# One more buffer for running totals in a causal attention kernel, paid for with smaller tiles of inverses

## The chip, the cores and the metric

The kernel runs on one core of one Trainium2 chip. The metric is device time in microseconds (us) from start to end of one launch, as the median of several runs.

## The reference, cut to what matters

```python
# x: (32, 256, 32, 32) f32; 8 heads of 32 channels, S = 1024 positions
xn = group_norm(x, 32 groups)
q, k, v = 1x1 convolutions of xn              # 256 channels each, with bias
scores = einsum('bhqd,bhkd->bhqk', q, k) / sqrt(32)
attn = softmax(where(k < q, scores, -1e4)); attn = where(k < q, attn, 0)
out = x + einsum('bhqk,bhkd->bhqd', attn, v)
```

## The kernel before: the parts that matter

A batch is one image. It is worked off in N = 12 visits. A visit multiplies q and k into `sT` (in PSUM, the on-chip memory for products; these are the score products), ScalarE takes exponentials of `sT` into the tiles `e` and `eh` (in SBUF, the on-chip memory for tiles), GpSimd masks the diagonal blocks, and one visit later TensorE multiplies them with v into `acc`. The heads come in two groups of four and the queries in two halves of 512, so a batch has four pairs, n = 0 to 3. The first exponentials of a pair go to a tile with tag `e0`, and VectorE adds all later ones of the pair onto it: this tile is the running total.

```python
epool = tc.alloc_tile_pool(name="epool", bufs=3)
...
tag = "e0" if full[2] == 0 else "e"        # k == 0: visits 0, 2, 6, 8 of a batch
e = epool.tile([P, 4, HALF], F32, tag=tag, name=f"{tag}_{name}")      # 8 KB a partition, 3 buffers
```

The 128 rows of a total are folded to 64 and then 32 by two adding DMAs issued on GpSimd. A plain DMA from SP's queue, called the stacking here, puts those 32 rows into `folded`; one product then sums all four pairs of the image. Only when the stacking has landed can the total's buffer be used again.

```python
def fold(b, n, rows):
    total = live["sum", b, *divmod(n, NH)]
    nc.gpsimd.dma_start(out=total[:rows], in_=total[rows : 2 * rows], accum_op=ALU.add)

def stack(b, n):
    if n == 0:
        live["folded", b] = work.tile([P, 4, HALF], F32, tag="folded", bufs=1, ...)
    total = live.pop(("sum", b, *divmod(n, NH)))
    nc.sync.dma_start(out=live["folded", b][n * HD : (n + 1) * HD], in_=total[:HD])
...
SUMS = (3, 7, 9, 13)                        # visit behind which pair n's first fold is asked for
PREPARE = (-18, -17, -16, -15, -14, -12, -11, -11)   # norm of an image: ..., mean, deviation, variance, ...
with tc.manual_schedule(engines={ENG.PE, ENG.Activation, ENG.DVE, ENG.Pool}):   # SP is not among them
    ...
    when(v, lambda b=b, n=n: fold(b, n, 2 * HD), after)
    when(v + 2, lambda b=b, n=n: fold(b, n, HD), after)
    when(v + 3, lambda b=b, n=n: stack(b, n), after)
    ...
    when(first + N + 6, lambda b=b: sum_folded(b), after)
```

`when(i, f)` runs f in visit i between its scores and its values, `after` behind its values; v is the visit behind which pair n's first fold is asked for (3, 7, 9, 13). The inverses of the sums come back from DRAM into `rb`, which also takes the finished output:

```python
live["rb", b] = work.tile([P, NG, S], F32, tag="rb", name=f"rb_{b}")    # 8 KB a partition, 2 buffers
```

Of the kernel before, what the change touches and what calls it, by code (L numbers as in the profile page):

```python
# [9 lines left out]
F32 = mybir.dt.float32  # L10
I32 = mybir.dt.int32
AF = mybir.ActivationFunctionType
# [5 lines left out]
P = 128  # L18
# [13 lines left out]
def tile_norm_attention_residual(  # L32
# [77 lines left out]
    def unshifted():  # L110
# [190 lines left out]
        def scores(b, full, half):  # L301


            tag = "e0" if full[2] == 0 else "e"
            name = f"{b}_{full[0]}_{full[1]}_{full[2]}"
            e = epool.tile([P, 4, HALF], F32, tag=tag, name=f"{tag}_{name}")
            eh = epool.tile([P, 4, HALFBANK], F32, tag="eh", bufs=4, name=f"eh_{name}")
            pairs = [ps_s.tile([P, 2, HALF], F32, tag="sT", name=f"sT_{name}_{a}") for a in range(3)]
            short = pairs[2].rearrange("p bank (n q) -> p bank n q", n=2)
            first = [scores_of((b, half), short[:, j % 2, 1, :], j) for j in (2, 3)]  # L310
            for j in range(4):
                scores_of((b, full), pairs[j // 2][:, j % 2, :], j)

            for ins in first:
                ins.then_inc(bank_free, 1)
                tc.no_tile_sem_insts.add(ins.ins.name)
            live["free"] = live.get("free", 0) + len(first)
            wait = nc.tensor.wait_ge(bank_free, live["free"])
            for ins in first:
                tc.declare_no_dep(wait.ins, ins.ins, reason="the semaphore orders them")  # L320
            for j in range(2):
                lo = scores_of((b, half), short[:, j, 0, :], j)
                for ins in first:
                    tc.declare_no_dep(lo.ins, ins.ins, reason="the semaphore orders them")
            for a in range(2):
                nc.scalar.activation(e[:, 2 * a : 2 * a + 2, :], pairs[a], AF.Exp)  # L326
            exp = nc.scalar.activation(eh.rearrange("p (n bank) q -> p bank n q", n=2), short, AF.Exp)  # L327

            for ins in first:
                tc.add_to_no_dep_group(f"first_{name}", ins.ins)  # L330
                tc.add_to_no_dep_group("first", ins.ins)
            tc.declare_no_dep(exp.ins, group=f"first_{name}", reason="through the last two products")
            tc.declare_fence(exp.ins, group=f"first_{name}")
            mask(full, e)
            mask(half, eh)
            live["e", b, full], live["e", b, half] = e, eh
# [30 lines left out]
        def stack(b, n):  # L367
            if n == 0:
                live["folded", b] = work.tile([P, 4, HALF], F32, tag="folded", bufs=1, name=f"folded_{b}")
            total = live.pop(("sum", b, *divmod(n, NH)))  # L370
            nc.sync.dma_start(out=live["folded", b][n * HD : (n + 1) * HD], in_=total[:HD])
# [64 lines left out]
        def invert(b, ns):  # L436
            part = slice(ns.start * HD, ns.stop * HD)
            inv = small.tile([P, ROW], F32, tag="inv", name=f"inv_{b}_{ns.start}")
            nc.vector.reciprocal(inv[part], live["rows", b][part])
            live["inv", b] = dram.tile([4, 4, HALF], F32, tag="inv", name=f"inverses_{b}_{ns.start}")  # L440
            nc.sync.dma_start(out=spread_rows(live["inv", b])[part], in_=inv[part])
            if ns.start == 0:
                live["rb", b] = work.tile([P, NG, S], F32, tag="rb", name=f"rb_{b}")
            by_half = live["inv", b] if b >= B - 2 else live["inv", b].rearrange("j n c -> n j c")
            for n in ns:
                g, hf = divmod(n, NH)
                nc.sync.dma_start(
                    out=live["rb", b][:, g, hf * HALF : (hf + 1) * HALF],
                    in_=by_half[n].unsqueeze(1).broadcast_to([4, HD, HALF]),
                )  # L450

        def finish(b, n, within=slice(0, HALF)):
            g, hf = divmod(n, NH)
            cols = slice(hf * HALF + within.start, hf * HALF + within.stop)
            num, rb, xt = live["num", b, n], live["rb", b], live["x", b]
            nc.vector.tensor_mul(rb[:, g, cols], num[:, within], rb[:, g, cols])  # L456
            nc.vector.scalar_tensor_tensor(  # L457
                rb[:, g, cols], rb[:, g, cols], v_bias_col[:, g : g + 1], xt[:, g, cols], ALU.add, ALU.add
            )
            if cols.start == 0:  # L460
                nc.vector.tensor_copy(rb[:, g, 0:1], xt[:, g, 0:1])
            nc.sync.dma_start(out=x_out[b, :, g, cols], in_=rb[:, g, cols])

        def check_here(n, ok):

# [3 lines left out]
            nc.vector.scalar_tensor_tensor(ok, live["most", n], SUM_MAX, least, ALU.is_le, ALU.mult)  # L469

        def invert_here(b, n, within):
            g, hf = divmod(n, NH)
            nc.vector.reciprocal(
                live["rb", b][:, g, hf * HALF + within.start : hf * HALF + within.stop], live["den", n][:, within]
            )

        def finish_aside(b, n):

            g, hf = divmod(n, NH)
            cols = slice(hf * HALF, (hf + 1) * HALF)  # L480
            num, rb, xt = live["num", b, n], live["rb", b], live["x", b]
            nc.gpsimd.tensor_tensor(rb[:, g, cols], num, rb[:, g, cols], ALU.mult)
            nc.gpsimd.tensor_tensor(rb[:, g, cols], rb[:, g, cols], xt[:, g, cols], ALU.add)
            nc.scalar.activation(rb[:, g, cols], rb[:, g, cols], AF.Identity, bias=v_bias_col[:, g : g + 1])
            if hf == 0:
                nc.scalar.copy(rb[:, g, 0:1], xt[:, g, 0:1])
            nc.sync.dma_start(out=x_out[b, :, g, cols], in_=rb[:, g, cols])

        def end_last(b):

# [33 lines left out]
        def when(i, f, where=at):  # L524
            where.setdefault(i, []).append(f)
# [22 lines left out]
        with tc.manual_schedule(engines={ENG.PE, ENG.Activation, ENG.DVE, ENG.Pool}):  # L548
# [23 lines left out]
            for b in range(B):  # L572
                first, last, late = b * N, b == B - 1, b >= B - 2
                if b >= 1:
                    for n, f in zip(PROJECT if not last else PROJECT[:-1] + (8,), projections(b)):
                        when(first + n, f)
                if b >= 2:
                    when(max(first - 2 * N + 3, 0), lambda b=b: load(b))
                    prepare(b, [first + n for n in PREPARE])
                for n in every:  # L580
                    v = first + (N if last and n == 3 else SUMS[n])
                    if last and n == 3:
                        for i in (N - 1, N):
                            when(first + i, lambda b=b, i=i: sum_pieces(b, products[i - 1], i == N - 1, i == N), after)
                    if late:
                        when(v, lambda b=b, n=n: sums(b, *divmod(n, NH)), after)
                    else:
                        when(v, lambda b=b, n=n: fold(b, n, 2 * HD), after)
                        when(v + 2, lambda b=b, n=n: fold(b, n, HD), after)
                        when(v + 3, lambda b=b, n=n: stack(b, n), after)  # L590
                if not last:
                    if not late:
                        when(first + N + 6, lambda b=b: sum_folded(b), after)
                    v = first + N + (2 if late else 8)
                    when(v, lambda b=b: gather(b, every))
                    when(v + 2, lambda b=b: check_sums(b, every))
                    when(v + 2, lambda b=b: invert(b, every))
                    for n in every:
                        when(first + FINISH[late][n], lambda b=b, n=n: finish(b, n), after)
                else:  # L600
                    when(first + N - 4, lambda b=b: gather(b, every[:2]))
                    when(first + N - 3, lambda b=b: check_sums(b, every[:2]))
                    when(first + N - 3, lambda b=b: invert(b, every[:2]))
                    when(first + N, lambda b=b: check_here(2, in_range[:, ROW : ROW + 1]))
                    when(first + N, lambda b=b: invert_here(b, 2, slice(0, HALF)))
                    when(first + N, lambda b=b: finish(b, 2))
                    for n in every[:2]:
                        when(first + N, lambda b=b, n=n: finish_aside(b, n), after)
# [167 lines left out]
```

## Time and profile before

| | before |
|---|---|
| median of the first three runs | 2074.72 us (2067.27 to 2076.96) |
| span of the profiled run | 2070.3 us |
| granted TensorE clock, mean | 0.958 |
| busy PE, DVE, ACT, POOL | 94%, 75%, 68%, 38% |

PE is TensorE's products, DVE is VectorE, ACT ScalarE, POOL GpSimd, SP the engine whose queue issues most DMAs. The page also gives the chain of work that ended last, as shares of the span by engine:

```profile
PE 62%; DMA 15%; ACT 8%; DVE 5%; POOL 5%; issue 4%; ACTq 0%; SPq 0%; POOLq 0%; DVEq 0%
```

Although PE is busy for 94% of the span, only 62% of the chain is PE's. Nearly all of the rest is a path around PE: masks, folds, stacking, exponentials.

### The profile page before, as it was taken

The numbers are of one execution on the slowest core, as the hardware profiler recorded it, in microseconds if no ns is written. First come the engines' busy times: TensorE is split into PE (matmuls) and PEld (weight loads), VectorE is DVE, ScalarE is ACT, GpSimd is POOL, SyncE is SP. The second block draws the span as 40 slices with busy tenths as digits, with TensorE's granted clock in tenths as the row PEclk, the third lists the DMA queues.
The fourth block names the chain that finished last, engine by engine and source line by source line (L and its number), as shares of the span: only waits on it lengthen the run. The fifth ranks groups of instructions, "written<-read, shape, count | busy, mean of one in ns | idle before, by whom it ended". The sixth has DMA issues, their size and how long they took to land.

```text
span 2070.3 us, 54028 instructions
## 1 busy us (share of the span) xinstructions
PE 1954.0 (94%) x23410; PEld 966.5 (47%) x23410; DVE 1562.8 (75%) x1604; ACT 1412.3 (68%) x1775; POOL 794.9 (38%) x741
## 2 busy tenths in 40 slices
PE   8999999999999999899999999999999999999996
PEld 4544444454444444445444454444444444544443
DVE  4787688777777877778777786787877777777767
ACT  5767676776667776667766676766776667766675
POOL 2444343442434434334343342443443434424323
PEclk9999999999999999999999999999999999999998
DMA  3555656656666556565556655656566555565412
GB/s 110 83 99 105 121 125 133 110 109 116 124 124 112 118 109 124 124 123 103 110 121 127 115 105 115 127 123 130 110 111 124 119 129 109 113 114 124 94 46 74
DMA packets 77660, 233.54 MB, mean 113 GB/s; under 512 B 19825, under 2 KB 20977, under 8 KB 62057
## 3 DMA queue, kind: packets, MB, share of 16 engines
q0 software_dynamic: 15360, 94.39, 33.9%
q1 hardware_dynamic: 60280, 134.72, 21.4%
q8 instruction: 185, 3.03, 0.7%
q10 hardware_dynamic: 1776, 0.92, 0.2%
q14 instruction: 59, 0.48, 0.1%
HBM read 68.54 MB, written 35.62 MB: 50 GB/s over the span
## 4 chain that ended last, share of the span: by engine, by line
PE 62%; DMA 15%; ACT 8%; DVE 5%; POOL 5%; issue 4%; ACTq 0%; SPq 0%; POOLq 0%; DVEq 0%
PE sT L279 22%; PE acc L349 15%; PE pp L171 11%; PE ppv L171 11%; DMA folded<-e 8%; DMA e<-e 6%; ACT e L326 6%; DVE e L354 4%; POOL e L294 2%; PE pd L384 2%; POOL eh L294 2%; ACT eh L327 2%; ACT k L233 1%; POOL rstd L209 1%; DVE rb L456 1%
## 5 line engine op out<-in xcount | busy, mean ns | idle before, releaser
L326 ACT ACTIVATE e<-sT 128x1024 f32<-128x1024 f32 x768 | 745.8, 1023 | 552.5 <-PE sT L279 325.6
L354 DVE TENSOR_TENSOR e<-e,eh 128x1024 f32<-128x1024 f32 x382 | 540.9, 1430 | 455.0 <-PE acc L349 429.8
L279 PE MATMUL sT<-q,k 32*128 32x256 f32 (+3 forms) x7168 | 679.9, 480 | 77.6 <-ACT e L326 76.8
L294 POOL TENSOR_SCALAR_AFFINE_SELECT e<-e 128x512 f32<-128x512 f32 (+1 forms) x256 | 365.5, 1428 | 877.1 <-ACT e L326 847.1
L354 DVE TENSOR_TENSOR e<-e,e 128x1536 f32<-128x1536 f32 x381 | 628.9, 1651 | 24.1 <-POOL e L294 3.0
L279 PEld LDWEIGHTS sT<-q,k 32*128 32x128 f32 x7168 | 478.2, 190 | 282.6 <-ACT e L326 96.6
L171 PE MATMUL pp<-xn,wT 128*32 128x512 f32 x4096 | 492.3, 598 | 0.0
L349 PE MATMUL acc<-e,v 128*32 128x512 f32 (+2 forms) x4096 | 400.7, 486 | 0.0
L327 ACT ACTIVATE eh<-sT 128x1024 f32<-128x1024 f32 x384 | 396.6, 1033 | 0.0
L365 POOL DMA_DIRECT2D e<-e x240 | 197.3, 861 | 363.7 <-DMA e<-e 227.6
L171 PE MATMUL ppv<-wT,xn 128*32 128x256 f32 x4096 | 274.3, 413 | 0.0
L349 PEld LDWEIGHTS acc<-e,v 128*32 128x32 f32 x4096 | 132.5, 110 | 224.8 <-issue 202.6
L349 PE MATMUL acc<-eh,v 128*32 128x256 f32 x3072 | 224.1, 379 | 0.0
L171 PEld LDWEIGHTS pp<-xn,wT 128*32 128x32 f32 x4096 | 107.0, 109 | 218.5 <-issue 205.6
L171 PEld LDWEIGHTS ppv<-wT,xn 128*32 128x32 f32 x4096 | 128.2, 118 | 134.5 <-issue 63.2
L294 POOL TENSOR_SCALAR_AFFINE_SELECT eh<-eh 128x512 f32<-128x512 f32 x128 | 178.3, 1393 | 0.4
L349 PEld LDWEIGHTS acc<-eh,v 128*32 128x32 f32 x3072 | 97.5, 110 | 165.3 <-issue 153.3
L456 DVE TENSOR_TENSOR rb<-num,rb 128x512 f32<-128x512 f32 (+1 forms) x127 | 110.9, 873 | 0.1
L457 DVE SCALAR_TENSOR_TENSOR rb<-rb,v_bias_col,x 128x512 f32<-128x512 f32 (+1 forms) x127 | 96.1, 757 | 4.5
L249 ACT COPY v<-ppv 128x512 f32<-128x512 f32 x128 | 77.3, 604 | 26.2 <-PE ppv L171 26.2
L233 ACT ACTIVATE q<-pp,qk_bias 128x512 f32<-128x512 f32 x128 | 89.8, 702 | 4.7 <-PE pp L171 4.7
L233 ACT ACTIVATE k<-pp,qk_bias 128x512 f32<-128x512 f32 x128 | 89.6, 700 | 2.2 <-PE pm L171 1.1
(69 smaller groups left out, 501.6 us busy)
## 6 DMA issues: line engine op xcount, KB each, us to landing
e<-e POOLq DMA_DIRECT2D x120, 512.0 KB, 7.9
x<-in_x_dram SPq DMA_DIRECT2D x64, 512.0 KB
out_dram<-rb SPq DMA_DIRECT2D x127, 256.0 KB
rb<-inverses SPq DMA_DIRECT2D x126, 256.0 KB
e<-e POOLq DMA_DIRECT2D x120, 256.0 KB, 4.6
folded<-e SPq DMA_DIRECT2D x120, 256.0 KB
rows<-sums SPq DMA_DIRECT2D x31, 32.0 KB
inverses<-inv SPq DMA_DIRECT2D x31, 32.0 KB
```

The source lines that it names most:

```text
L171: nc.tensor.matmul(out[part], lhsT=lhsT[:, part], rhs=rhs, start=start, stop=stop, skip_group_check=True)
L233: nc.scalar.activation(live[key][:, cols], pp, AF.Identity, bias=qk_bias[:, n, g : g + 1], scale=(SCALE, 1.0)[n],)
L249: nc.scalar.copy(live["v", b][:, 2 * n : 2 * n + 2, :], pp)
L279: ins = nc.tensor.matmul(pair[:, cols], lhsT=live["k", b, g][rows, kb * P : (kb + 1) * P], rhs=live["q", b, g][rows, hf * HALF + of.start ...
L294: nc.gpsimd.affine_select(out=diagonal, in_=diagonal, pattern=[[0, 4], [0, n], [1, P]], compare_op=ALU.is_gt, fill=0.0, base=0, channel_mu ...
L326: nc.scalar.activation(e[:, 2 * a : 2 * a + 2, :], pairs[a], AF.Exp)
L327: exp = nc.scalar.activation(eh.rearrange("p (n bank) q -> p bank n q", n=2), short, AF.Exp)
L349: nc.tensor.matmul(acc[HD * j : HD * (j + 1), of], lhsT=live["v", b][:, kb, h * HD : (h + 1) * HD], rhs=e[:, j, cols], start=first, stop=l ...
L354: nc.vector.tensor_add(total[:, :, of], total[:, :, of], e[:, :, cols])
L365: nc.gpsimd.dma_start(out=total[:rows], in_=total[rows : 2 * rows], accum_op=ALU.add)
L456: nc.vector.tensor_mul(rb[:, g, cols], num[:, within], rb[:, g, cols])
L457: nc.vector.scalar_tensor_tensor(rb[:, g, cols], rb[:, g, cols], v_bias_col[:, g : g + 1], xt[:, g, cols], ALU.add, ALU.add)
```

## The change

It gives the running totals a fourth buffer (8 KB a partition). Room for it comes from `rb`: a tile of 2 KB for each pair, four of them, instead of two tiles of 8 KB for a whole image. And it asks for each stacking two visits behind the second fold (`v + 4`), not one (`v + 3`, after the values). Without the smaller `rb` the fourth buffer doesn't fit; the build then says that its pool needs 72 KB a partition and 71.06 are left.

```diff
-            e = epool.tile([P, 4, HALF], F32, tag=tag, name=f"{tag}_{name}")
+            e = epool.tile([P, 4, HALF], F32, tag=tag, bufs=4 if tag == "e0" else 3, name=f"{tag}_{name}")
...
-            if ns.start == 0:
-                live["rb", b] = work.tile([P, NG, S], F32, tag="rb", name=f"rb_{b}")
...
+        def inverses(b, n):
+            live["rb", b, n] = work.tile([P, HALF], F32, tag="rb", bufs=4, name=f"rb_{b}_{n}")
+            return live["rb", b, n]
...            (finish, invert_here and finish_aside use live["rb", b, n] in the same way)
-                        when(v + 3, lambda b=b, n=n: stack(b, n), after)
+                        when(v + 4, lambda b=b, n=n: stack(b, n))
```

## The prediction

> **What bounds the kernel now.** I read the page first, then the waits, the chain, PE's timeline around one wait, and last the sums over chosen windows. The page puts PE first, and the granted clock at full almost everywhere:
>
> ```profile
> PE 1954.0 (94%) x23410; PEld 966.5 (47%) x23410; DVE 1562.8 (75%) x1604; ACT 1412.3 (68%) x1775; POOL 794.9 (38%) x741
> ```
>
> PE is the bound. Its missing 6% and the half-speed time hidden in its busy time are what can be won. The table of waits, over the whole span, says what it waits for:
>
> ```profile
> ACT e L326 <- DMA folded<-e: 179.9, 33, 8.8
> PEld sT L279 <- ACT e L326: 96.6, 57, 5.8
> PE sT L279 <- ACT e L326: 76.8, 38, 5.5
> ```
>
> Read them backwards. PE's score products wait for PSUM that the exponentials free; the exponentials wait, 33 times, some once a batch (32 images), for the DMA that stacks a running total's 32 rows into `folded` (the stacking). Only then is the total's buffer free for the next one. In the chain of waits one such event looks like this (start, length, what):
>
> ```profile
> 1035.84 1.62 POOL eh L294
> 1037.46 7.21 DMA e<-e
> ...
> 1044.80 6.82 DMA folded<-e
> ...
> 1051.72 1.03 ACT e L326
> ...
> 1052.80 3.84 PE sT L279 x12
> ```
>
> The second fold (an adding DMA issued by GpSimd) takes 7.21 us, the stacking 6.82 us, the exponential 1.03 us, and then PE goes on. PE's timeline shows the price:
>
> ```profile
> 1052.80 3.91 PE L279 MATMUL sT<-q,k 32*128 32x256 f32 x16 [3.85 <-ACT e L326]
> 1056.64 2.95 PE L171 MATMUL ppv<-wT,xn 128*32 128x256 f32 x32
> ...
> 1061.24 1.57 PE L279 MATMUL sT<-q,k 32*128 32x256 f32 x16
> 1062.74 1.93 PE L171 MATMUL ppv<-wT,xn 128*32 128x256 f32 x32
> ```
>
> PE stood for 3.85 us, and then the same two groups took 3.91 and 2.95 us where one visit later they take 1.57 and 1.93. The wait is paid twice: as idle time and as a slow restart.
>
> **Which wait it is.** A batch has 12 visits (each starts with a group of score products in PE's timeline). A running total starts at visits 0, 2, 6, 8. With three buffers, the total of visit 2 takes the one of the previous batch's visit 6, whose folds are due after visits 9 and 11 and whose stacking after visit 12, which is this batch's visit 0. So the stacking has two visits to land, and it doesn't. The trace agrees: the wait ends before the scores of visit 3, and once, in the batch from 1544.83, there is one at visit 6 instead.
>
> **What the Trainium skill says.** "TensorE: Matmul & The Clock Gate", Part 1, has the array run at half clock after an idle window of some 3.4 us and return after a busy one. The trace agrees on the restart: 0.89 is granted in the idle window below and 0.55 in the 6.60 us after it. It also pays after shorter waits; see the batch mean below. "DMA: Bandwidth & Descriptors", Issuing engines are not separate DMA queues, says that all transfers run on the same 16 engines and interleave. The trace agrees: the DMA share is 0.68 and then 1.02 around the wait, against 0.53 for the rest of the batch (windows below); that is why 256 KB of stacking needs 6.82 us. "Perfetto Trace Analysis", DMA Instruction — HWDGE, says that the movement is not in the reported time of the issue; so I read landings from who waits.
>
> **The change part by part.** Windows: us, then busy time (instructions) of PE, PEld, DVE, ACT, POOL, then granted clock, DMA share, GB/s.
>
> ```profile
> 80.45:138.39 57.94, 57.56 (x732) 29.23 (x728) 42.12 (x41) 43.81 (x55) 24.52 (x24) 1.00 0.50 78
> 138.39:1929.27 1790.88, 1701.61 (x20389) 839.76 (x20385) 1368.91 (x1401) 1228.53 (x1540) 704.98 (x645) 0.96 0.60 118
> ...
> 1048.90:1052.80 3.90, 0.05 (x5) 0.00 (x1) 3.87 (x6) 1.08 (x2) 0.79 (x1) 0.89 0.68 204
> 1052.80:1059.40 6.60, 6.60 (x48) 3.20 (x52) 1.05 (x2) 5.68 (x7) 0.80 (x1) 0.55 1.02 196
> 1059.40:1113.90 54.50, 54.12 (x684) 27.04 (x676) 43.78 (x44) 37.15 (x47) 23.39 (x21) 1.00 0.53 101
> ```
>
> The first window is batch 1, which has no such wait, at full clock: 57.94 us. The second holds 28 batches (2 to 29): 1790.88 / 28 = 63.96 us each. So the wait with its restart costs 63.96 - 57.94 = 6.02 us a batch; the single event above costs 3.85 + (3.91 + 2.95 - 1.57 - 1.93) = 7.2 us, and some are smaller.
>
> 1. *Fourth buffer.* Each total now takes the buffer of the same total a batch ago. The slack from stacking to reuse becomes 5, 3, 5 and 3 visits of some 4.8 us, even with the stacking put one visit later. Measured from the second fold's issue (1037.46) to the stacking's landing (1051.62) there are 14.2 us, under three visits, so I expect the wait gone in all batches. Gain: 28 x 6.02 = 168.6 us, and in batch 30, whose visits 2 and 3 I read from PE's timeline as 6.34 and 8.64 us against 4.22 and 5.09 in batch 1, another 5.7 us. Sum 174.3 us.
> 2. *Room.* `rb` goes from 2 x 8 KB to 4 x 2 KB, the new total costs 8 KB: even. The number and size of instructions and transfers stay; a half's `rb` is used from visit 10 to visit 2 of the next batch, and its slot is asked for again at visit 10. No wait; 0 us. Only the end, where inverses of the last image are wanted two visits after the image before, could wait a little: I take 1 us.
> 3. *Stacking later.* No instruction is added. A stacking waits on SP for its fold anyway; it now stands behind some loads of inverses and some output stores in that in-order queue, so it may land some us later, inside the new slack. 0 us.
>
> What stays: DVE has 48.8 us of work a batch (1562.8 us over 32 batches), 84% of 57.94; ACT has 44.1 us, 76%.
>
> **Rivals.** *A. The sum product becomes the wait.* After visit 6 PE multiplies `folded`, so it needs the stacking of the last total, issued in visit 3 or 4 among image loads and stores. Today the stall before it gives it time. The batch that lost the stall shows how near it is (ACT's, SP's and PE's timelines):
>
> ```profile
> 1577.77 1.94 ACT L326 ACTIVATE e<-sT 128x1024 f32<-128x1024 f32 x2 [3.77 <-DMA folded<-e]
> 1566.93 16.93 SPq L371 DMA_DIRECT2D folded<-e  x2
> 1581.25 1.93 PE L384 MATMUL pd<-folded,pick_half 128*32 128x512 f32 x8 [2.48 <-ACT k L233]
> ```
>
> That stacking was issued at 1566.93 and landed at 1577.77, after 10.8 us; PE was ready for the sum product at 1581.25 - 2.48 = 1578.77, 1.0 us later. (It waited there through ACT, which stood at visit 6; the fourth buffer removes that.) This batch still lost 6.20 - 5.09 = 1.1 us at visit 3, so without it the margin is about nothing. For: the product stays at its visit, and the change makes nothing of the last total's path shorter. Against: it costs only the overlap. I take 0.4 us a batch, 28 x 0.4 = 11 us. If stackings land 1.5 us later, with some half-clock restarts, it is 50 to 60 us, and the time about 1955.
>
> *B. DVE becomes the bound.* For: 84% busy, and its finishing work lies in visits 0 to 3, where the stall used to let it catch up. Against: in that same batch without a stall at visit 2 it was waiting for PE again by 1563.98, before visit 4. I give it 0; if it came, 1 us a batch, about 1935.
>
> *C. The wait shifts to another transfer or to GpSimd*, which stands 7 us in front of the second fold with masks behind it. For: 227.6 us of its waits are for the folds. Against: visits 2 and 3 have no masks, and in that batch GpSimd was free at 1563.45, visit 4's mask came at 1567.85. If it took back half the gain, the time would be near 1990.
>
> **Range and chances.** 2074.7 - 174.3 + 1 + 11 = 1912. The floor without any new wait is 1901 and some noise; hence the low end 1893. Rival A at twice to four times my size gives 1925 to 1945, the upper end. Nothing in the change adds work, so slower is nearly excluded; within 2% (above 2033) would need over two thirds of the gain given back.
>
> **What would show each step right or wrong.** Right: the waits of ACT for `folded` gone or under 10 us; batches 2 to 29 at 58 to 59 us; no score product waiting more than 1 us for ACT; granted clock above 0.98; busy time of DVE, ACT and POOL the same, PE's down by the restarts (some 80 us). Rival A shows as idle before the sum product, once a batch, and cold visits at 7. B shows as values or exponentials waiting for DVE's sums, C as exponentials or values waiting for GpSimd. The prediction is wrong if the exponentials still wait for `folded`, most likely because a stacking behind other entries of SP's queue comes more than three visits late.

## The result

| | before | changed |
|---|---|---|
| median of 4 runs | 2075.84 us (2067.27 to 2077.10) | 1901.83 us (1901.16 to 1902.73) |
| span of the profiled run | 2070.3 us | 1900.5 us |
| granted clock, mean | 0.958 | 0.997 |
| PE busy | 1954.0 us (94%) | 1860.3 us (98%) |

The ratio of times is 0.917, with a 95% interval of 0.9145 to 0.9196. Ratios here are the mean time of one kernel's runs over that of the other's of the same rounds, so they aren't quite the ratio of the quoted medians. The kernel before varies by about 1.5% from run to run in the studies below (2053 to 2083 us), the changed one by some 0.3%.

From the page of the changed kernel, the busy times and the chain:

```profile
PE 1860.3 (98%) x23410; PEld 944.9 (50%) x23410; DVE 1569.0 (83%) x1604; ACT 1410.1 (74%) x1775; POOL 802.5 (42%) x741
...
PE 89%; ACT 5%; DMA 2%; issue 2%; DVE 1%; POOL 0%; ACTq 0%; POOLq 0%; SPq 0%; DVEq 0%
```

PE executes the same 23410 products in 93.7 us less busy time; busy time before included products that ran at half clock. By the trace's record of the granted clock, which is 0.5 or 1.0 at any moment, PE was busy during 148 of the 174 us at half clock, so the clock accounts for at most half of that, 74 of the 93.7 us (an estimate from this record). The DMA's share of the chain fell from 15% to 2%. The table of waits no longer has the line of exponentials waiting for `folded`; these are what is left of it and beside it:

```profile
ACT e L326 <- PE sT L279: 359.7, 347, 1.8
...
PE pm L171 <- ACT k L233: 11.4, 30, 0.4
...
PE pd L384 <- DMA folded<-e: 1.1, 3, 0.5
```

The exponentials now wait mostly for PE, so ScalarE follows PE and not the reverse. PE itself still stands 0.38 us once a batch before the product that gives the means (`pm`), and now and then shortly before the product over `folded` (`pd`).

PE's timeline, in one batch, at visits 2 (612.58), 3 (616.80) and 4 (621.88); compare the restart that the prediction shows:

```profile
612.58 1.57 PE L279 MATMUL sT<-q,k 32*128 32x256 f32 x16
614.08 1.92 PE L171 MATMUL pp<-xn,wT 128*32 128x512 f32 x16
615.82 1.05 PE L349 MATMUL acc<-e,v 128*32 128x384 f32 x16
616.80 1.57 PE L279 MATMUL sT<-q,k 32*128 32x256 f32 x16
618.30 1.93 PE L171 MATMUL ppv<-wT,xn 128*32 128x256 f32 x32
```

No line has an idle time before it, and the score products take 1.57 us. The window of batches 2 to 29, with the columns that the prediction explains:

```profile
138.02:1764.48 1626.46, 1612.32 (x20388) 818.76 (x20385) 1375.92 (x1401) 1226.46 (x1540) 713.30 (x645) 1.00 0.66 130
```

1626.46 / 28 = 58.09 us a batch, against 63.96 before.

All later readings of visits come from PE's timeline: a visit starts with its first score product, twelve make a batch. These are means over batches 2 to 29, in us, of each kernel's profiled run:

| kernel | batch | visit 2 | visit 3 | visit 6 | clock |
|---|---|---|---|---|---|
| before | 63.96 | 6.88 | 8.24 | 5.85 | 0.958 |
| changed | 58.09 | 4.22 | 5.09 | 5.81 | 0.997 |
| `rb_alone` | 63.47 | 6.73 | 7.95 | 5.83 | 0.964 |
| `four_stack_soon` | 58.14 | 4.22 | 5.09 | 5.87 | 0.996 |
| `three_fold_sooner` | 62.29 | 5.74 | 7.42 | 6.17 | 0.979 |
| `hold8` | 59.33 | 4.23 | 6.47 | 5.67 | 0.997 |
| `hold14` | 64.29 | 6.85 | 8.80 | 5.67 | 0.958 |
| `hold20` | 66.55 | 9.46 | 8.46 | 5.67 | 0.942 |

Of the 6.02 us a batch over 57.94, the kernel before lost 2.66 in visit 2, 3.15 in visit 3 and 0.18 in visit 6. The changed kernel has visits 2 and 3 at their floor in each of these batches, and visit 6 takes 0.14 us more than its floor of 5.67.

### The profile page after: what moved, and what is told of

Same layout as the page of the kernel before. It is cut to its first block, busy times and chain, and to the rows that moved or that the text cites. A ratio compares the mean times of both kernels' runs of the same rounds, so it can differ in the third digit from the quotient of the medians.

```text
span 1900.5 us, 54083 instructions
## 1 busy us (share of the span) xinstructions
PE 1860.3 (98%) x23410; PEld 944.9 (50%) x23410; DVE 1569.0 (83%) x1604; ACT 1410.1 (74%) x1775; POOL 802.5 (42%) x741
## 4 chain that ended last, share of the span: by engine, by line
PE 89%; ACT 5%; DMA 2%; issue 2%; DVE 1%; POOL 0%; ACTq 0%; POOLq 0%; SPq 0%; DVEq 0%
PE sT L279 29%; PE acc L349 24%; PE pp L171 21%; PE ppv L171 12%; ACT e L326 2%; PE pd L384 2%; ACT eh L327 1%; DMA folded<-e 1%; ACT k L233 1%; DVE e L354 0%; PE pm L171 0%; DMA wn<-in_L_conv_kv_w_dram 0%; DVE rb L472 0%; DVE rb L457 0%; DVE rb L458 0%
## 5 line engine op out<-in xcount | busy, mean ns | idle before, releaser
L294 POOL TENSOR_SCALAR_AFFINE_SELECT e<-e 128x512 f32<-128x512 f32 (+1 forms) x256 | 387.1, 1512 | 698.1 <-ACT e L326 673.9
L354 DVE TENSOR_TENSOR e<-e,e 128x1536 f32<-128x1536 f32 x381 | 638.4, 1676 | 25.0 <-POOL e L294 4.0
L279 PE MATMUL sT<-q,k 32*128 32x256 f32 (+3 forms) x7168 | 617.5, 460 | 0.8 <-ACT k L233 0.8
L279 PEld LDWEIGHTS sT<-q,k 32*128 32x128 f32 x7168 | 463.4, 184 | 170.5 <-ACT q L233 50.6
L365 POOL DMA_DIRECT2D e<-e x240 | 197.4, 862 | 364.8 <-DMA e<-e 205.9
L171 PE MATMUL ppv<-wT,xn 128*32 128x256 f32 x4096 | 247.3, 382 | 0.0
L171 PEld LDWEIGHTS ppv<-wT,xn 128*32 128x32 f32 x4096 | 120.2, 109 | 102.0 <-issue 32.1
L294 POOL TENSOR_SCALAR_AFFINE_SELECT eh<-eh 128x512 f32<-128x512 f32 x128 | 164.0, 1281 | 1.1
L357 ACT COPY num<-acc 128x512 f32<-128x512 f32 x128 | 76.4, 597 | 15.9 <-PE acc L349 15.9
```

What stands on the lines that cost most here:

```text
L171: nc.tensor.matmul(out[part], lhsT=lhsT[:, part], rhs=rhs, start=start, stop=stop, skip_group_check=True)
L279: ins = nc.tensor.matmul(pair[:, cols], lhsT=live["k", b, g][rows, kb * P : (kb + 1) * P], rhs=live["q", b, g][rows, hf * HALF + of.start ...
L294: nc.gpsimd.affine_select(out=diagonal, in_=diagonal, pattern=[[0, 4], [0, n], [1, P]], compare_op=ALU.is_gt, fill=0.0, base=0, channel_mu ...
L354: nc.vector.tensor_add(total[:, :, of], total[:, :, of], e[:, :, cols])
L357: nc.scalar.copy(num, acc)
```

## The experiments

The theory: the gain is the removal of one wait, that of the exponentials for a total's buffer, and the wait was paid as idle time and again as a slow restart. The rivals: the smaller tiles or the place of the stacking did something; the slow products came of crowded DMAs; more buffers weren't needed, only an earlier fold.

### `rb_alone`: everything but the fourth buffer

```diff
-bufs=4 if tag == "e0" else 3
+bufs=3
-                        when(v + 4, lambda b=b, n=n: stack(b, n))
+                        when(v + 3, lambda b=b, n=n: stack(b, n), after)
```

> The changed kernel with three buffers of totals and the old place of the stacking: only the smaller tiles of inverses are left of the change. Theory (the fourth buffer is the whole gain): 2076 us, within 1% of the kernel before; exponentials wait some 180 us for folded again. Rival (the smaller tiles free something): clearly under 2050 us.

Measured: 2068.72 us, ratio 1.0012 (0.9944 to 1.0081), the same as the kernel before. Its table of waits has the old line:

```profile
ACT e L326 <- DMA folded<-e: 168.7, 32, 9.0
```

The smaller tiles change nothing measurable by themselves. They are the room and nothing else.

### `four_stack_soon`: the fourth buffer, the stacking in its old place

```diff
-                        when(v + 4, lambda b=b, n=n: stack(b, n))
+                        when(v + 3, lambda b=b, n=n: stack(b, n), after)
```

> The changed kernel with the stacking asked for where the kernel before had it, after visit v+3. Built, its order of instructions and waits on every engine is the same as that of the changed kernel but for buffer numbers. Theory: the place of that line does nothing, 1902 us within 0.3%. Rival (the prediction's part 3, that the stackings move behind loads and stores in SP's queue): the stackings' issue times differ by some us, and the time by a few us.

Measured: 1903.25 us, ratio 0.9184 (0.9132 to 0.9235); the changed kernel's is 0.917. Comparing the built instruction lists engine by engine, I found this kernel and the changed one the same in order and waits, and SP's order of transfers the same in the kernel before as well; the traces agree, with the same order of SP's 539 transfers, by tile names, in all three. SP isn't among the engines whose order the source fixes, so moving the line by a visit moved no instruction. The prediction had said that the stackings would now stand behind loads of inverses and stores in SP's queue. The third total's stacking does, behind four such loads and one store, but it stood there in the kernel before already.

### `hold8`, `hold14`, `hold20`: the wait rebuilt without a DMA

These are the changed kernel with idle copies put in ScalarE's queue ahead of visit 2's exponentials, in batches 2 to 29. Nothing waits for a buffer; the exponentials are just late.

```diff
+        held = const.tile([P, HALFBANK], F32, name="held")
+        def hold(count):
+            for _ in range(count):
+                nc.scalar.copy(held, wT[:, 0, :HALFBANK])
...
+                if 2 <= b < B - 2:
+                    when(first + 1, lambda: hold(8), after)      # 14, 20 in the others
```

> The changed kernel with 8 copies of 128x256 put on ScalarE ahead of visit 2's exponentials in batches 2 to 29, some 0.3 us each, 2.4 us in all: about 1.2 us more than the idle time that stands there. Theory and rival alike: that fits into the room before PE waits, under 10 us in all, 1902 to 1912 us. It fixes the zero of the two longer holds.

> 14 such copies, some 4.2 us, 3.0 us over the idle time there. Theory (a wait of PE is paid twice, as idle time and as a restart at half clock): PE stands about 1 us a batch and in part of the batches some 3 us of slow restart follow; 1950 to 2020 us. Rival (only the idle time is paid): 1902 + 28 x 1 = 1930 us, clock as before near 1.

> 20 such copies, some 6 us, 4.8 us over the idle time there. Theory: PE stands about 3 us a batch, and then some 3.3 us go to half clock; 1902 + 28 x 6.3 = 2078 us, granted clock near 0.96, the kernel before over again without any DMA in it. Rival (the slow restart came of the crowded DMA or of something else in the kernel before): idle alone, 1902 + 28 x 3 = 1986 us, clock near 0.99.

Measured: `hold8` 1934.87 us (ratio 0.9364), `hold14` 2072.88 (1.0029), `hold20` 2137.10 (1.0341). The copies were longer than I had reckoned: 8 took 3.49 us and 14 took 6.10 by ScalarE's timeline, some 0.44 us each and not 0.3. So each hold is larger than its expectation assumed, and all three missed their numbers; `hold14`, with 4.59 us of delay as measured below, came out where `hold20` had been expected (4.8 us, 2078 us). Counted from the start of visit 2, the first exponential of it begins at 1.19 us in the changed kernel and at 3.16, 5.78 and 8.39 in the three, delays of 1.97, 4.59 and 7.20 us. In the kernel before it begins at 5.79 us on average, as in `hold14`, which was luck and makes the two easy to compare. The cost a batch over 57.94 us is 1.39, 6.35 and 8.61.

PE's timeline in `hold8`, at visit 3:

```profile
624.02 0.70 PE L279 MATMUL sT<-q,k 32*128 32x256 f32 x4
624.93 2.04 PE L279 MATMUL sT<-q,k 32*128 32x512 f32 x12 [0.21 <-ACT e L326]
626.90 1.93 PE L171 MATMUL ppv<-wT,xn 128*32 128x256 f32 x32
```

And in `hold14`:

```profile
666.78 0.70 PE L279 MATMUL sT<-q,k 32*128 32x256 f32 x4 [2.56 <-ACT e L326]
667.69 2.99 PE L279 MATMUL sT<-q,k 32*128 32x512 f32 x12 [0.21 <-ACT e L326]
670.61 3.64 PE L171 MATMUL ppv<-wT,xn 128*32 128x256 f32 x32
```

In `hold8` the score products are strung out along the exponentials: they take 624.02 to 626.90, 2.88 us, instead of 1.50, with hardly a gap to be seen, and the next products run at full speed (1.93 us for 32). The clock stays at 0.997. In `hold14` PE stands 2.56 us as well and afterwards the same 32 products take 3.64 us. The windows of its wait and of the 6.83 us from 667.54 (clock, DMA share and GB/s are the last three numbers) show why:

```profile
664.22:666.78 2.56, 0.00 (x2) 0.00 (x1) 2.56 (x4) 2.46 (x6) 0.00 (x0) 1.00 0.89 201
667.54:674.37 6.83, 6.68 (x48) 3.12 (x52) 1.58 (x3) 4.97 (x8) 1.34 (x2) 0.50 0.91 122
```

The half clock is granted after the wait. Over batches 2 to 29 the clock record has such stretches, of 3.41 or 6.83 us each, in every batch of `hold14`, in 26 of the 28 of the kernel before and in none of `hold8`. In `hold14` the cost exceeds the delay, 6.35 against 4.59 us. From `hold14` to `hold20` it rises by 2.26 us for 2.61 us of delay, so the restart is not paid again. The mean clock still falls, to 0.942, because more of the half clock falls into the wait itself: PE was busy during 168 of its 232 us, against 159 of 160 in `hold14`. So the mean clock alone is no measure of the cost.

`hold14` has the fourth buffer and no wait for any DMA, and yet its time (ratio 1.0029 to the kernel before), its clock (0.958) and its visits 2 and 3 are nearly those of the kernel before. So neither the number of buffers nor a wait for a DMA is needed for the slow products; a late exponential does it. The DMA engines were crowded there too (0.91), so `hold14` alone doesn't rule out that crowding slows the products. The window of one stacking in the kernel before speaks against it:

```profile
1044.80:1051.62 6.82, 4.15 (x48) 1.86 (x48) 6.73 (x10) 0.00 (x0) 0.28 (x1) 1.00 0.92 228
```

At a DMA share of 0.92 and a clock of 1.00, the score products at 1044.66 took 1.57 us and the 16 products behind them 1.92, as in the changed kernel.

### `three_fold_sooner`: three buffers, the one fold a visit earlier

```diff
-bufs=4 if tag == "e0" else 3
+bufs=3
-                        when(v + 2, lambda b=b, n=n: fold(b, n, HD), after)
-                        when(v + 4, lambda b=b, n=n: stack(b, n))
+                        when(v + (1 if n == 2 else 2), lambda b=b, n=n: fold(b, n, HD), after)
+                        when(v + (2 if n == 2 else 3), lambda b=b, n=n: stack(b, n), after)
```

> Three buffers, but the second fold of the third total (started at visit 6) is asked for one visit earlier, and its stacking with it. Theory (it is the lateness of that one stacking, not the count of buffers as such): the stacking is issued some 6 us sooner and the wait at visits 2 and 3 goes. What is left is the next one in line with three buffers, the stacking of the last total before visit 6, some 3 us short as in the batch at 1544.83 of the kernel before; so batches of 59.5 to 62 us, 1945 to 2015 us in all, 1975 as the point. Rival (the fold itself would be as late, because GpSimd's queue or the shared DMA engines set it): no change, 2060 to 2090 us.

Measured: 2023.89 us, ratio 0.9785 (0.9726 to 0.9844), just outside what I expected and a quarter of the gain (the interval excludes 1). Its waits still have a large line:

```profile
ACT e L326 <- DMA folded<-e: 156.7, 41, 9.8
```

The fold was issued when I had reckoned: on average 10.7 us after visit 9 begins instead of 16.8, and the stacking followed at 17.5 instead of 23.8. But it landed at 28.4 instead of 29.7, by the landings that the trace records. Its way took 10.9 us instead of 5.9. SP's timeline shows what it stands behind now:

```profile
1009.29 4.15 SPq L444 DMA_DIRECT2D rb<-inverses  x4
1013.64 1.68 SPq L371 DMA_DIRECT2D folded<-e  x1
1021.01 10.82 SPq L461 DMA_DIRECT2D out_dram<-rb  x4
```

Directly ahead of it are the four loads of inverses, 1 MB in all; in the kernel before they were issued 10 us or more earlier (1031.82 to 1034.38, the stacking at 1044.80). That these loads cost the 5 us is argued from this order; no run moved them, and none issued the stacking from another engine's queue. What is shown is that this earlier issue brought almost no earlier landing: what the schedule won, the transfer lost. The fourth buffer doesn't make the transfer faster; it makes its lateness harmless.

### `sum_early` and `sum_late`: how much room the next edge has

The changed kernel with the product over `folded` after visit 5 or visit 7 of the next batch, instead of 6.

```diff
-                        when(first + N + 6, lambda b=b: sum_folded(b), after)
+                        when(first + N + 5, lambda b=b: sum_folded(b), after)      # N + 7 in sum_late
```

> The changed kernel with the sum product of folded one visit earlier, after visit 5. Theory (the last total's stacking lands some 27.7 us after visit 1 begins, so the product at 28.1 has no room left, and one visit earlier it is 4.6 us short): PE waits some 4.3 us a batch and restarts at half clock, 7 to 8 us a batch, 2095 to 2130 us. Rival (the stackings have more room than it looks and land when they are asked for): 1900 to 1910 us.

> The sum product one visit later, after visit 7. Theory: the waits of 0.1 to 0.8 us before it, 4 us in the profile over 28 batches, go: 1896 to 1900 us, and nothing else waits for the sums. Rival (the later sums make the check, the inverses and VectorE late): above 1905 us.

Measured: `sum_early` 2076.64 us (ratio 1.0042), `sum_late` 1896.09 (0.9167). One visit earlier costs the whole gain: batches of 64.31 us, of which visit 5 takes 10.87. My range for it began some 20 us too high. One visit later, all 28 batches are within 0.01 us of 57.87 us and the waits before `pd` are gone. In the changed kernel the last total's stacking lands on average 27.7 us after visit 1 begins (the stackings that land in batches 2 to 29), and PE is ready for the product at 28.2. So the change stopped 0.4 us short of the next wait, on average, and in single batches (0.1 to 0.8 us) it met it.

PE's timeline in `sum_early` shows the same pattern at another place, in one of the milder batches:

```profile
1070.20 1.06 PE L384 MATMUL pd<-folded,pick_half 128*32 128x512 f32 x8 [2.21 <-issue]
1071.19 2.94 PE L279 MATMUL sT<-q,k 32*128 32x256 f32 x16
```

PE stands 2.21 us (the profile names no releaser for this one) and the score products behind it take 2.94 us instead of 1.57. The restart isn't always paid: in the batch from 266.43 PE stood 3.52 us before `pd`, the clock stayed at 1.00 and the score products behind took 1.57 us.

### `mean_moved`, `both_moved`, and the two runs again on one chip

The last regular gap is the 0.38 us before `pm`. It waits for ScalarE's copy of k out of the one PSUM bank that small products and projections share. After visit 10 that bank holds v instead, copied earlier.

```diff
-        PREPARE = (-18, -17, -16, -15, -14, -12, -11, -11)
+        PREPARE = (-18, -17, -14, -14, -13, -12, -11, -11)
```

> The product that gives the means moved from after visit 8, where it waits for the copy of k out of the one shared PSUM bank, to after visit 10, where v's copy frees it; the variance product one visit later. Theory: the gaps of 0.38 us, one a batch, go: 30 x 0.38 = 11 us, 1888 to 1894 us. Rival (the bank is freed as late there too, or the normalised image comes late): 1900 us or more.

> Both moves together. Theory: they add, 1884 to 1891 us, PE busy over 98.5% of the span. Rival: one eats the other, as in mean_moved.

> The changed kernel itself once more, as the measure for mean_again on the same chip. Theory: 1902 us within 0.3%, batches 2 to 29 at 58.1 us in the profile.

> mean_moved once more, on the same chip as the changed kernel. Theory: 0.55 us a batch less (visit 8 at 4.22 instead of 4.84 us, visit 11 at 4.82 instead of 4.75), 17 us or 0.9% under after_again. Rival (the gain was a difference of chips): within 0.3% of it.

Measured: `mean_moved` 1884.11 us (ratio 0.9111), `both_moved`, which is it with `sum_late`, 1887.89 (0.9124). On one chip, `after_again` took 1903.06 us (1901.04 to 1906.15) and `mean_again` 1884.40 (1882.41 to 1886.18): `mean_moved` beats both kernels, by 18.7 us over the changed one. The product before the move, in the changed kernel, after visit 8:

```profile
994.86 0.24 PE L171 MATMUL pm<-mv,avg 128*32 128x2 f32 x8 [0.38 <-ACT k L233]
```

And in `mean_moved`, after visit 10:

```profile
993.72 0.24 PE L171 MATMUL pm<-mv,avg 128*32 128x2 f32 x8
```

The gain was larger than the 11 us expected, outside the range, because visit 8 lost the gap and the product itself (4.84 to 4.22 us), visit 10 kept its length since the variance product left it, and visit 11 grew by 0.07 us only. `both_moved` lies inside its expected range and yet refutes its theory: the two moves don't add, and together they are 3.8 us slower than `mean_moved` alone. With the sums a visit later, the variance product of `both_moved` waits for VectorE in 10 batches, 6.3 us in its table of waits, and visit 11 grows from 4.82 to 5.09 us on average. That VectorE is late because the check of the sums stands ahead of it in its queue is what the order in the source suggests; VectorE's table has 10 waits, 21.5 us, for the rows of the sums, of which `mean_moved` has none. No run tested it.

## Why the prediction was right, point by point

The prediction gave 1912 us and 1893 to 1945; 1901.83 was measured. That it came within 10 us is in part luck: its base, 2074.7 us, is one draw from a kernel that varies between 2053 and 2083. The comparison batch by batch doesn't depend on that.

1. **The bound and the wait** were read right. The wait of exponentials for `folded` is gone from the table, visits 2 and 3 are at the floor in batches 2 to 29, and `rb_alone` and `four_stack_soon` together show that the fourth buffer does it. One reading was loose: the stacking doesn't have two visits to land. It waits for the second fold and is issued 23.8 us after visit 9 begins, just when visit 2 begins, and lands 5.9 us later. That shared DMA engines are why it needs so long was argued; what the trace shows is that during one stacking the engines moved 228 GB/s in 6.82 us, about six times its 256 KB.
2. **The gain a batch** was put at 6.02 us, from the batch that had no such wait. Measured: 63.96 - 58.09 = 5.87; the rest is the waits before `pd`. Batch 30 gave 64.70 - 59.89 = 4.8 us and not 5.7: its visit 3 has the product `pd<-e` more (5.95 us), which the comparison with batch 1 overlooked. The 1 us set aside for the end wasn't needed: 76.3 us before and 76.1 after, from the end of batch 30. Taking the clean batch as the floor was worth more than adding up single waits: it contains all forms of the cost.
3. **Paid twice**: right as a sum, coarse in its parts. `hold14` repeats the cost with no wait for a DMA in it. `hold8` shows a third form, score products strung out at full clock, 1.38 us in visit 3, that the prediction had counted as slow restart. The half clock can account for at most 70.6 us over batches 2 to 29 (half the time that PE was busy at it, by the clock record), 2.5 a batch, less than the 3.15 us lost in visit 3. How strung-out and half-clock products share the visit when both occur isn't settled. And the restart after shorter waits, which the prediction read from the batch mean, is in the clock record: in the batch from 267.24 of the kernel before, gaps of 0.69 and 0.22 us were followed by 3.41 us at half clock.
4. **Room**: right, 0 us, by `rb_alone`.
5. **Stacking later**: the time was right, 0 us, the reason wrong. The prediction took the source's order for SP's order. `four_stack_soon`, the built lists and the traces show that no transfer changed its place in SP's queue.
6. **Rival A**, the product over `folded`, was put at 0.4 us a batch, 11 us. It measured 58.09 - 57.94 = 0.15 us a batch, 4 us. This is the mis-sized term, and most of the 10 us between 1912 and 1902. Its mechanism is real, as `sum_early` shows: the margin is 0.4 us.
7. **Rivals B and C** didn't come. VectorE is 83% busy, as reckoned (84%), and GpSimd's waits for folds are 205.9 us in the table of waits, against 227.6.

## What to carry to other kernels

When a buffer's release runs through a slow transfer, look for a batch in the trace that happened not to wait; its length is the floor, and the difference is what one more buffer can bring, idle time and slow restart together. Before asking for the transfer earlier, find out whether its issue or its way is slow: here an issue 6 us earlier landed only 1.3 us earlier. And check in the built order that moving a line of source moves an instruction at all.

## What the Trainium skill lacked or had wrong

- "TensorE: Matmul & The Clock Gate", Part 1, ties the half clock, in its table of two states, to at least one idle window of some 3.4 us. In `hold14` PE's gaps were 2.56 and some 0.2 us a batch, and half clock followed in all 28; in the kernel before, gaps of 0.69 and 0.22 us were enough in the batch from 267.24. Gaps clearly shorter than the window can be enough, then, and 3.52 us in the batch from 266.43 of `sum_early` were not. (Idle time inside a strung-out group of products doesn't show as a gap here.) The same part does say of another kernel that frequent short idles made the clock go back and forth, but gives no lengths.
- "DMA: Bandwidth & Descriptors", Anatomy of one DMA, fits a time of 2.0 us and the bytes over 436 GB/s for a DMA issued by GpSimd; as an estimate from it, 2.6 us for 256 KB and 3.2 for 512 KB. The adding folds, which GpSimd issues here, took 4.6 and 7.9 us (medians on the page of both kernels). I found no such fit for SP's queue, nor a number for transfers among others: the stacking of the third total took 5.9 us on average in the kernel before, that of the last one 10.3 us, and the third's took 10.9 us behind 1 MB of loads in `three_fold_sooner`.
- No page that I read has the case of `hold8`: products that are released piece by piece show almost no gap and cost 1.38 us a visit. "Trainium Kernel Development and Optimization", Performance Expectations, does warn that busy time of products is a bad metric; this case agrees, with 1954.0 and 1860.3 us for the same 23410 products.
